# Second half of the gated state by way of DRAM, and a shorter lead of the attention

## The chip, the cores and the metric

The kernel runs on one core of a Trainium2 chip. A core has engines that run side by side, each with its own in-order queue of instructions: TensorE (PE, matrix products; its weight loads are shown as PEld), VectorE (DVE), ScalarE (ACT), GpSimd (POOL) and SyncE (SP, which here only issues DMAs). TensorE writes into PSUM, which has eight banks of 128 x 512 floats; everything else works in SBUF, and DMA engines move data between SBUF and DRAM. The metric is the device time of one execution in microseconds (us), lower is better. The kernel before takes 2796.8 us, the median of three runs (2795.94 to 2798.14).

## The reference

128 graphs of 128 nodes with 256 features pass through four residual layers. The first three are graph attention, the last is a gated graph network with three steps:

```
# layers 0, 1, 2, each with its own W and a
h = relu(layernorm(x))
Wh = h @ W
e = leaky_relu((Wh @ a1)[:, :, None] + (Wh @ a2)[:, None, :], 0.2)
x = x + elu(softmax(where(adj > 0, e, -9e15)) @ Wh)
# layer 3
h = relu(layernorm(x)); A = (adj != 0)
for i in range(3):
    aggr = einsum('bst,bsd->btd', A, h @ weight[i])
    gi = aggr @ w_ih.T + b_ih; gh = h @ w_hh.T + b_hh
    r = sigmoid(i_r + h_r); z = sigmoid(i_z + h_z); n = tanh(i_n + r * h_n)
    h = (1 - z) * n + z * h
x = x + h
```

All of it is in 32-bit floats.

## The kernel before, in words

**Groups.** The graphs are cut into 33 groups: two of 2 graphs at the ends and 31 of 4 graphs between. For each group `gat` (L661) records three attention layers and the norm ahead of the gated steps, and `gru` (L727) records the three gated steps and the output.

**Attention** (`attention`, L482): norm and scores on VectorE and ScalarE, softmax, then the sums of neighbours (`ahp`, L618) and the product with W (`hp`, L637) on TensorE. From group 2 on, the attention weights are transposed without TensorE: VectorE transposes blocks of 32 x 32, one DMA writes the tile to DRAM and four DMAs read the blocks back in their new places (`exchanged`, L429). A row of scores is spread over the partitions by two DMAs (`de`, `er`).

**A gated step** (`step`, L764). The state h is kept with features in the partitions ("feature-major"), in two halves of 128 features, k or c = 0 and 1. Half c of the new state needs six products with `whh` on the old state and six with `wc` on the aggregated state `ag` (`product`, L774, at L780), into the PSUM tiles nn, r, z and ni. ScalarE and VectorE then form r, n, z, the differences d and the new half `h` (L835 to L872). The aggregation (`agp`, L805) needs the old state the other way round, with nodes in the partitions, called `hn`; `ag` is its copy (L813). All this runs over the four graphs of the group at once, 512 columns.

**Two ways to `hn`.** For the second half (k = 1), and for both halves in groups 0, 1, 31 and 32, `node_major` (L749) lets TensorE transpose each graph's 128 x 128 piece into the PSUM tile hnp (L753), and ScalarE copies it out (L794). For the first half of groups 2 to 30 `turned_state` (L460) is used as soon as that half of h exists (L875 to L877): a block transpose on VectorE (L467), a write to DRAM (L470), four reads back (L474). The tile `hn0` of the next step is kept in the list `ahead` until that step takes it.

**PSUM.** `BANKS` (L232) gives two banks to the attention, five to the gated products and one, "tr", to `hnp` and `agp` together.

**What sets the order.** No order is written out by hand. `Plan` (L40) collects every operation with an engine, an estimated cost, a rank and its dependencies, and then plays the program through with those estimates (`issue`, L108): at each turn an engine takes, among the operations that can start within 0.1 us of the earliest (WINDOW), the one of lowest rank. An operation can't be taken while its rank is more than 6 (AHEAD) above the lowest unfinished one. The resulting order is what the engines get; on the chip each engine follows it and waits where the data isn't there yet. A DMA is an operation of SP with a cost of 0.45 us, after which its data are taken to land `lands` us later (L56); `LANDS` = 6.0 (L212) is that time for the reads of `turned_state`. Rank counts gated steps: step i of group g has rank 3g + i, its vector and scalar work a rank lower by 2 (URGENT), and layer l of the attention has 3g - lead + 2l (L485). `lead` (L916) is how many gated steps ahead of its own gated steps a group's attention begins: 8.5 for groups 0 and 1, 8.0 for the others.

Of the kernel before, what the change touches and what calls it, by code (L numbers as in the profile page):

```python
# [181 lines left out]
def kernel(  # L182
# [26 lines left out]
    B, N, D = x.shape  # L209
    KD = D // P  # L210
    G = 4
    LANDS = 6.0  # L212
    FAR = 2
    SIZES = [2] + [G] * ((B - 4) // G) + [2]
    NG = len(SIZES)
# [244 lines left out]
    def turned_state(src, dst, name, n, rank):  # L460


        tr = val(gw, "trs", [G, P], f"tr_{name}", cut=n)
        d = plan.val(
            dram, f"ds_{n}", 2, lambda: dram.tile([n, P, P], FT, tag=f"ds_{n}", name=f"d_{name}")
        )
        add("DVE", dve(n * P), rank, lambda: nc.vector.transpose(  # L467
            tr.t.rearrange("p b j -> p (b j)"), src.t[:, : n * P]
        ), reads=[src], writes=[tr], takes=[d, dst])
        load(3.0, rank, lambda: nc.sync.dma_start(d.t.rearrange("b p f -> p b f"), tr.t),  # L470
            reads=[tr], writes=[d])

        def back(j):
            load(LANDS, rank, lambda: nc.sync.dma_start(  # L474
                dst.t[j * 32 : (j + 1) * 32, : n * P].rearrange("c (m r) -> c m r", r=32),
                d.t[:, :, j * 32 : (j + 1) * 32].rearrange("b (q c) r -> c (b q) r", q=Q),
            ), reads=[d], writes=[(dst, j)])

        for j in range(Q):
            back(j)  # L480
# [246 lines left out]
    def gru(g, xt, am, hn0, h0):  # L727
# [35 lines left out]

        def step(i):  # L764
            name = f"{g}_{i}"
            rank = 3.0 * g + i
            quick = rank - URGENT
            ag = [state(f"ag{k}", f"ag_{name}_{k}") for k in range(KD)]
            hn = [
                ahead[0] if k == 0 and ahead else state(f"hn{k}", f"hn_{name}_{k}")  # L770
                for k in range(KD if i > 0 else 0)
            ]

            def product(ps, c, w, v, k, start, stop, at, takes=(), after=after):  # L774
                def fn():
                    if v is None:
                        o, m = cut(ps.t[:, :TG]), first(k)
                    else:
                        o, m = ps.t[:, :TG], v.t[:, :TG]
                    nc.tensor.matmul(  # L780
                        o, w.t[:, k, c * P : (c + 1) * P], m, start=start, stop=stop
                    )
                return add("PE", 2 * (0.005 + TG / 1200), at, fn,
                    reads=[w, h0 if v is None else v], writes=[ps], after=after, takes=takes)

            def aggregate(k):

                if i > 0:
                    hv = hn[k]
                    if k == 0 and ahead:  # L790
                        ahead.clear()
                    else:
                        hp = node_major(name, h[k], k, rank + 0.1 * k, hv)
                        add("ACT", act(TG), quick, lambda: nc.scalar.copy(  # L794
                            hv.t[:, :TG], hp.t[:, :TG]), reads=[hp], writes=[hv])
                ps = bank("tr", f"agp_{name}_{k}")
                t = ag[k]

                def part(b):
                    def fn():  # L800
                        if i > 0:
                            s = hv.t[:, b * P : (b + 1) * P]
                        else:
                            s = hn0.t[:, b, k * P : (k + 1) * P]
                        nc.tensor.matmul(  # L805
                            ps.t[:, b * P : (b + 1) * P], s, am.t[:, b, :], start=True, stop=True
                        )
                    add("PE", pe(P), rank + 0.1 * k, fn,
                        reads=[hv if i > 0 else hn0, am], writes=[(ps, b)], after=after, takes=[t])

                for b in range(n_g):
                    part(b)
                add("DVE", dve(TG), quick, lambda: nc.vector.tensor_copy(t.t[:, :TG], ps.t[:, :TG]),  # L813
                    reads=[ps], writes=[t])

            def half(c):
                at = rank + 0.2 + 0.3 * c
                cr, cz, cn = c, KD + c, 2 * KD + c
                nn, pr, pz, ni = (bank("gru", f"{v}_{name}_{c}") for v in ("nn", "r", "z", "ni"))
                wn, r, n, z, d = (state(v, f"{v}_{name}_{c}") for v in ("wn", "r", "n", "z", "d"))  # L820
                hc = state(f"h{c}", f"h_{name}_{c}")
                takes = [wn, r, n, z, d, hc, *(ag + hn if c == 0 else ())]
                begun = list(after)
                for k in range(KD):
                    early = rank + 0.1 * k if c == 0 else at
                    ops = [
                        product(nn, cn, whh, h[k], k, k == 0, k == KD - 1, early, takes),
                        product(pr, cr, whh, h[k], k, k == 0, False, early, takes),
                        product(pz, cz, whh, h[k], k, k == 0, False, early, takes),
                    ]  # L830
                    if k == 0:
                        begun += ops
                    if c == 0:
                        aggregate(k)
                add("ACT", act(TG) + 0.1, quick, lambda: nc.scalar.activation(  # L835
                    wn.t[:, :TG], nn.t[:, :TG], AF.Identity, bias=bh.t[:, cn : cn + 1]
                ), reads=[nn, bh], writes=[wn])
                for k in range(KD):
                    product(pr, cr, wc[i], ag[k], k, False, k == KD - 1, at)
                add("ACT", act(TG) + 0.1, quick, lambda: nc.scalar.activation(  # L840
                    r.t[:, :TG], pr.t[:, :TG], AF.Tanh, bias=brz.t[:, cr : cr + 1], scale=0.5
                ), reads=[pr, brz], writes=[r])
                add("DVE", dve(TG), quick, lambda: nc.vector.scalar_tensor_tensor(  # L843
                    n.t[:, :TG], r.t[:, :TG], 1.0, wn.t[:, :TG], op0=OP.add, op1=OP.mult
                ), reads=[r, wn], writes=[n])
                for k in range(KD):
                    product(ni, cn, wc[i], ag[k], k, k == 0, k == KD - 1, at, after=begun)
                add("DVE", dve(TG), quick, lambda: nc.vector.tensor_add(  # L848
                    n.t[:, :TG], ni.t[:, :TG], n.t[:, :TG]), reads=[ni, n], writes=[n])
                add("ACT", act(TG) + 0.1, quick, lambda: nc.scalar.activation(  # L850
                    n.t[:, :TG], n.t[:, :TG], AF.Tanh, bias=bi.t[:, cn : cn + 1]
                ), reads=[n, bi], writes=[n])
                for k in range(KD):
                    product(pz, cz, wc[i], ag[k], k, False, k == KD - 1, at)
                add("ACT", act(TG) + 0.1, quick, lambda: nc.scalar.activation(
                    z.t[:, :TG], pz.t[:, :TG], AF.Tanh, bias=brz.t[:, cz : cz + 1], scale=0.5
                ), reads=[pz, brz], writes=[z])

                hv = h[c]

                def difference():
                    if hv is None:
                        nc.vector.tensor_sub(cut(d.t[:, :TG]), first(c), cut(n.t[:, :TG]))
                    else:
                        nc.vector.tensor_sub(d.t[:, :TG], hv.t[:, :TG], n.t[:, :TG])

                add("DVE", dve(TG), quick, difference,
                    reads=[h0 if hv is None else hv, n], writes=[d])
                add("DVE", dve(TG), quick, lambda: nc.vector.scalar_tensor_tensor(  # L869
                    d.t[:, :TG], z.t[:, :TG], 1.0, d.t[:, :TG], op0=OP.add, op1=OP.mult  # L870
                ), reads=[z, d], writes=[d])
                add("DVE", dve(TG), quick, lambda: nc.vector.scalar_tensor_tensor(  # L872
                    hc.t[:, :TG], d.t[:, :TG], 0.5, n.t[:, :TG], op0=OP.mult, op1=OP.add
                ), reads=[d, n], writes=[hc])
                if c == 0 and i < STEPS - 1 and FAR <= g < NG - FAR:  # L875
                    ahead.append(state("hn0", f"hn_{g}_{i + 1}_0"))
                    turned_state(hc, ahead[0], f"hn_{g}_{i + 1}", n_g, quick)  # L877
                return hc

            return [half(c) for c in range(KD)]  # L880

        for i in range(STEPS):
# [32 lines left out]

    def lead(g):  # L916

        return 8.5 if g < FAR else 8.0

    for g in range(NG):  # L920
        gru(g, *gat(g))
# [37 lines left out]
```

## Time and profile before

| what | value |
|---|---|
| time, median of 3 | 2796.8 us |
| span of the profiled run | 2799.5 us |
| TensorE busy | 2744.8 us, 9789 matmul instructions |
| VectorE busy | 2188.9 us, 5680 instructions |
| ScalarE busy | 1207.8 us, 2569 instructions |
| GpSimd busy | 293.9 us, 369 instructions |
| DMA | 215.67 MB in 350398 packets, 157200 of them under 512 bytes |
| mean granted TensorE clock | 0.995 |

A busy time is the time in which at least one instruction of the engine is shown at work. A matmul's end is modelled, and consecutive matmuls overlap in the picture, so the mean duration of one is longer than what it costs in a full queue. A row "A <- B" among the waits says that A's engine stood idle until B ended; the same sign in an instruction's name stands between what it writes and what it reads. A 32-bit product counts as two matmul instructions in the profile, a transpose as one.

### The profile page before, as it was taken

The numbers are of one execution on the slowest core, as the hardware profiler recorded it, in microseconds if no ns is written. First come the engines' busy times: TensorE is split into PE (matmuls) and PEld (weight loads), VectorE is DVE, ScalarE is ACT, GpSimd is POOL, SyncE is SP. The second block draws the span as 40 slices with busy tenths as digits, with TensorE's granted clock in tenths as the row PEclk, the third lists the DMA queues.
The fourth block names the chain that finished last, engine by engine and source line by source line (L and its number), as shares of the span: only waits on it lengthen the run. The fifth ranks groups of instructions, "written<-read, shape, count | busy, mean of one in ns | idle before, by whom it ended". The sixth has DMA issues, their size and how long they took to land.

```text
span 2799.5 us, 32211 instructions
## 1 busy us (share of the span) xinstructions
PE 2744.8 (98%) x9789; PEld 1592.6 (57%) x9789; DVE 2188.9 (78%) x5680; ACT 1207.8 (43%) x2569; POOL 293.9 (10%) x369
## 2 busy tenths in 40 slices
PE   6899999999999999999999999999999999999998
PEld 4755555555555555555555555555555555555546
DVE  7879878778787878887878888788887888877544
ACT  4444444444443444444444444444444444444323
POOL 1111010010110101110100111010110110100000
PEclk9999999999999999999999999999999999999999
DMA  3113323333223333223233223232223233222210
GB/s 101 53 53 99 84 74 84 92 86 91 75 68 83 86 92 86 71 66 91 85 92 85 66 78 87 79 95 84 65 74 93 81 95 83 59 61 79 60 33 12
DMA packets 350398, 215.67 MB, mean 77 GB/s; under 512 B 157200, under 2 KB 318992, under 8 KB 350224
## 3 DMA queue, kind: packets, MB, share of 16 engines
q1 hardware_dynamic: 350224, 213.60, 28.1%
q8 instruction: 78, 1.28, 0.2%
q14 instruction: 96, 0.79, 0.1%
HBM read 124.85 MB, written 88.66 MB: 76 GB/s over the span
## 4 chain that ended last, share of the span: by engine, by line
PE 84%; DVE 9%; DMA 3%; ACT 2%; SPq 1%; issue 1%; POOL 0%; DVEq 0%; ACTq 0%
PE r L780 20%; PE z L780 20%; PE hp L637 11%; PE ni L780 10%; PE nn L780 10%; PE agp L805 5%; PE ahp L618 5%; DVE scr L506 1%; DMA d_o<-tr_o 1%; PE hnp L753 1%; DVE d L869 1%; DVE n L848 1%; DVE h L872 1%; DVE n L843 1%; DMA d_h<-tr_h 1%
## 5 line engine op out<-in xcount | busy, mean ns | idle before, releaser
L780 PE MATMUL nn<-h,whh 128*128 128x512 f32 (+1 forms) x792 | 397.8, 584 | 6.4 <-DVE h L872 6.4
L780 PE MATMUL r<-ag,wc 128*128 128x512 f32 (+1 forms) x792 | 396.6, 582 | 0.9 <-DVE ag L813 0.9
L780 PE MATMUL z<-h,whh 128*128 128x512 f32 (+1 forms) x792 | 395.9, 581 | 0.4 <-ACT r L840 0.4
L780 PE MATMUL r<-h,whh 128*128 128x512 f32 (+1 forms) x792 | 395.9, 581 | 0.0
L780 PE MATMUL z<-ag,wc 128*128 128x512 f32 (+1 forms) x792 | 394.3, 579 | 0.0
L780 PE MATMUL ni<-ag,wc 128*128 128x512 f32 (+1 forms) x792 | 393.8, 579 | 0.0
L637 PE MATMUL hp<-w,ah 128*128 128x256 f32 x1536 | 374.1, 383 | 0.7 <-ACT ah L625 0.5
L637 PEld LDWEIGHTS hp<-w,ah 128*128 128x128 f32 x1536 | 279.5, 190 | 61.9 <-issue 18.4
L506 DVE SCALAR_TENSOR_TENSOR scr<-xn,va 128x256 f32<-128x256 f32 x732 | 270.7, 424 | 29.7 <-ACT xn L498 29.4
L840 ACT ACTIVATE r<-r,brz 128x512 f32<-128x512 f32 (+1 forms) x198 | 132.9, 671 | 350.6 <-PE r L780 350.0
L780 PEld LDWEIGHTS r<-ag,wc 128*128 128x128 f32 x792 | 147.6, 190 | 181.3 <-issue 154.7
L780 PEld LDWEIGHTS z<-h,whh 128*128 128x128 f32 x792 | 150.1, 191 | 176.9 <-issue 165.4
L805 PEld LDWEIGHTS agp<-am,hn 128*128 128x128 f32 x1536 | 206.6, 192 | 73.4 <-issue 41.6
L780 PEld LDWEIGHTS r<-h,whh 128*128 128x128 f32 x792 | 151.5, 191 | 167.2 <-issue 158.7
L780 PEld LDWEIGHTS ni<-ag,wc 128*128 128x128 f32 x792 | 145.7, 190 | 149.5 <-issue 137.5
L566 ACT ACTIVATE em<-em,nmx 128x128 f32<-128x128 f32 x384 | 149.5, 391 | 187.8 <-DVE nmx L562 187.7
L780 PEld LDWEIGHTS z<-ag,wc 128*128 128x128 f32 x792 | 145.8, 190 | 148.7 <-issue 147.3
L843 DVE SCALAR_TENSOR_TENSOR n<-r,wn 128x512 f32<-128x512 f32 (+1 forms) x198 | 132.0, 667 | 119.9 <-ACT r L840 119.3
L805 PE MATMUL agp<-am,hn 128*128 128x128 f32 x1536 | 210.2, 276 | 12.7 <-DVE ag L813 8.3
L651 ACT ACTIVATE t<-hp 128x512 f32<-128x512 f32 x192 | 104.6, 594 | 267.0 <-PE hp L637 266.8
L618 PEld LDWEIGHTS ahp<-at,xn 128*128 128x128 f32 x1536 | 188.8, 194 | 47.7 <-issue 40.4
L780 PEld LDWEIGHTS nn<-h,whh 128*128 128x128 f32 x792 | 142.9, 191 | 121.3 <-issue 101.9
(91 smaller groups left out, 3508.6 us busy)
## 6 DMA issues: line engine op xcount, KB each, us to landing
er<-de SPq DMA_DIRECT2D x90, 256.0 KB, 4.1
d_at<-tr_at SPq DMA_DIRECT2D x90, 256.0 KB, 2.0
at<-d_at SPq DMA_DIRECT2D x360, 64.0 KB, 2.0
x<-in_x_dram SPq DMA_DIRECT2D x31, 512.0 KB, 3.9
d_h<-tr_h SPq DMA_DIRECT2D x31, 512.0 KB, 3.0
h<-d_h SPq DMA_DIRECT2D x124, 128.0 KB, 3.5
out_dram<-xo SPq DMA_DIRECT2D x31, 512.0 KB, 2.8
d_o<-tr_o SPq DMA_DIRECT2D x30, 512.0 KB, 5.3
```

The costliest lines, as they stand in the source:

```text
L506: add("DVE", dve(D), rank, lambda: nc.vector.scalar_tensor_tensor(scr.t, xn.t[:, b, :], 1.0 if far else rs.t[:, b : b + 1], VA[l].t[:, s, ...
L566: add("ACT", 0.42, rank, lambda: nc.scalar.activation(em.t[:, b, :], em.t[:, b, :], AF.Exp, bias=nmx.t[:, b : b + 1], accum_out=sm.t[:, b ...
L618: add("PE", pe(P), rank, lambda: nc.tensor.matmul(summed(ps, b), xn.t[:, b, k * P : (k + 1) * P], turned_weights(b), start=True, stop=True ...
L637: add("PE", pe(D), rank, lambda: nc.tensor.matmul(hp.t[:, b * D : (b + 1) * D], ah.t[:, k, c * P : (c + 1) * P], W[l].t[:, k, :], start=(k ...
L651: power = add("ACT", act(T), rank, lambda: nc.scalar.activation(t.t, hp.t, AF.Exp), reads=[hp], writes=[t])
L753: add("PE", 0.11, rank, lambda: nc.tensor.transpose(ps.t[:, b * P : (b + 1) * P], hv.t[:, b * P : (b + 1) * P], ident), reads=[hv], writes ...
L780: nc.tensor.matmul(o, w.t[:, k, c * P : (c + 1) * P], m, start=start, stop=stop)
L805: nc.tensor.matmul(ps.t[:, b * P : (b + 1) * P], s, am.t[:, b, :], start=True, stop=True)
L840: add("ACT", act(TG) + 0.1, quick, lambda: nc.scalar.activation(r.t[:, :TG], pr.t[:, :TG], AF.Tanh, bias=brz.t[:, cr : cr + 1], scale=0.5) ...
L843: add("DVE", dve(TG), quick, lambda: nc.vector.scalar_tensor_tensor(n.t[:, :TG], r.t[:, :TG], 1.0, wn.t[:, :TG], op0=OP.add, op1=OP.mult), ...
L848: add("DVE", dve(TG), quick, lambda: nc.vector.tensor_add(n.t[:, :TG], ni.t[:, :TG], n.t[:, :TG]), reads=[ni, n], writes=[n])
L869: add("DVE", dve(TG), quick, lambda: nc.vector.scalar_tensor_tensor(d.t[:, :TG], z.t[:, :TG], 1.0, d.t[:, :TG], op0=OP.add, op1=OP.mult), ...
```

## The change

The second half of the state takes the way through DRAM as well, in the same groups 2 to 30. `half(c)` calls `turned_state` for both c, and `ahead` now holds both tiles. So the 58 steps concerned have no transposes on TensorE, no copies on ScalarE, and twice the block transposes and DMAs. `ahead` is emptied before the halves are recorded, and the flag `through` says whether a step has both tiles.

The planner's numbers change with it: the write of `turned_state` is taken to land after 2.6 us (3.0 before), its reads after 2.8 (6.0 before), and a product of 512 columns to cost 0.006 us less. The attention of groups from 2 on begins 6.5 gated steps ahead in place of 8.0. The purpose is to take the remaining transposes off TensorE, with the attention's products placed where the gated steps wait for the state.

```diff
-    LANDS = 6.0
@@ turned_state
-        load(3.0, rank, lambda: nc.sync.dma_start(d.t.rearrange("b p f -> p b f"), tr.t),
+        load(2.6, rank, lambda: nc.sync.dma_start(d.t.rearrange("b p f -> p b f"), tr.t),
             reads=[tr], writes=[d])
         def back(j):
-            load(LANDS, rank, lambda: nc.sync.dma_start(
+            load(2.8, rank, lambda: nc.sync.dma_start(
@@ step
+            through = bool(ahead)
             hn = [
-                ahead[0] if k == 0 and ahead else state(f"hn{k}", f"hn_{name}_{k}")
+                ahead[k] if ahead else state(f"hn{k}", f"hn_{name}_{k}")
                 for k in range(KD if i > 0 else 0)
             ]
@@ product
-                return add("PE", 2 * (0.005 + TG / 1200), at, fn,
+                return add("PE", 2 * (0.002 + TG / 1200), at, fn,
@@ aggregate
-                    if k == 0 and ahead:
-                        ahead.clear()
-                    else:
+                    if not through:
                         hp = node_major(name, h[k], k, rank + 0.1 * k, hv)
@@ half
-                if c == 0 and i < STEPS - 1 and FAR <= g < NG - FAR:
-                    ahead.append(state("hn0", f"hn_{g}_{i + 1}_0"))
-                    turned_state(hc, ahead[0], f"hn_{g}_{i + 1}", n_g, quick)
+                if i < STEPS - 1 and FAR <= g < NG - FAR:
+                    ahead.append(state(f"hn{c}", f"hn_{g}_{i + 1}_{c}"))
+                    turned_state(hc, ahead[c], f"hn_{g}_{i + 1}_{c}", n_g, quick)
                 return hc
+            ahead.clear()
             return [half(c) for c in range(KD)]
@@ lead
-        return 8.5 if g < FAR else 8.0
+        return 8.5 if g < FAR else 6.5
```

## The prediction

> **What bounds the kernel now.** I read the page's busy times first, then the table by stretches of 100 us, then what TensorE waited for, and last the chain of waits in the middle of the run.
>
> ```profile
> PE 2744.8 (98%) x9789; PEld 1592.6 (57%) x9789; DVE 2188.9 (78%) x5680; ACT 1207.8 (43%) x2569; POOL 293.9 (10%) x369
> ```
>
> TensorE is busy in 2744.8 of 2799.5 us and VectorE in 78%. A mean doesn't say where the 54.7 us are lost; the table by stretches does (columns: stretch, length, busy time of PE, PEld, DVE, ACT and POOL with instruction counts, granted clock, DMA share, GB/s):
>
> ```profile
> 0.00:100.00 100.00, 73.96 (x337) 56.75 (x338) 76.13 (x269) 46.03 (x127) 17.67 (x30) 0.93 0.29 84
> 100.00:200.00 100.00, 91.24 (x383) 62.43 (x382) 78.22 (x233) 44.84 (x108) 13.50 (x17) 0.97 0.22 59
> 1000.00:1100.00 100.00, 100.00 (x339) 55.29 (x339) 83.05 (x216) 44.06 (x91) 11.90 (x14) 1.00 0.31 80
> 2700.00:2800.00 100.00, 90.53 (x347) 57.59 (x345) 38.72 (x72) 27.83 (x52) 0.00 (x0) 0.98 0.04 14
> ```
>
> The first 200 us lose 34.8 us and the last 100 lose 9.5. All of 200 to 2700 loses about 10 us. So from 200 us on the end is set by the amount of TensorE work, and a TensorE instruction taken away there is worth its slot. The waits of TensorE agree: the first two of these touch the state between steps, the third the attention's way through DRAM, and all are small (columns: total us, times, longest).
>
> ```profile
> PE nn L780 <- DVE h L872: 6.4, 7, 2.8
> PE agp L805 <- ACT hn L794: 4.5, 7, 0.7
> ...
> PE ahp L618 <- DMA at<-d_at: 1.2, 1, 1.2
> ```
>
> The removed work in the groups of instructions (busy us, mean ns):
>
> ```profile
> L753 PE MATMUL hnp<-ident,h 128*128 128x128 f32 x292 | 45.2, 275 | 3.4 <-DVE h L872 3.0 <-DVE ag L813 0.3
> L794 ACT COPY hn<-hnp 128x512 f32<-128x512 f32 (+1 forms) x74 | 41.5, 561 | 83.9 <-PE hnp L753 83.8
> L467 DVE STREAM_TRANSPOSE tr_hn<-h 128x512 f32<-128x512 f32 x58 | 41.3, 711 | 2.0
> ```
>
> The 275 ns are not the price of a transpose, since its modelled end overlaps the next. The chain of waits shows the slot of four (start, us):
>
> ```profile
> 1219.87 0.44 PE hnp L753 x4
> 1220.30 0.86 PE ni L780 x2
> ```
>
> 0.44 us for four, 0.11 each, with TensorE work on both sides.
>
> **What the Trainium skill says.** "Perfetto Trace Analysis", Identifying the Most-Contended Engine: matmul busy share is no measure of the distance to the limit, because the instructions are pipelined. The trace agrees: 275 ns shown, 110 ns of slot. I therefore count slots. "VectorE: DVE Perf Modes", The three transpose paths: VectorE transposes only within 32x32 blocks. That is why the new route needs the passage through DRAM to move the blocks; the trace has one such pass at 711 ns. "DMA: Bandwidth & Descriptors", Rules for kernel authors: a DMA that reads what another wrote must wait for its completion before it is issued. In the trace the four reads indeed start only 2.3 us after the write. The same page, Latency and other measured facts, gives HBM latency as 0.2 us on average and 2 us at high load, which I use only as an upper bound.
>
> **The change, part by part.**
>
> Removed from TensorE. Groups 2 to 30 (29 of them) have two steps that read a state of the step before: 58 times four transposes of the second half, 232 instructions. In the order of the built programs the transposes fall from 292 to 60 and nothing else on TensorE changes in number. 58 x 0.44 = 25.5 us, all in the stretch where TensorE is full. Removed from ScalarE: 58 copies of about 0.58 us, 34 us of an engine at 43%: nothing.
>
> Added to VectorE: 58 block transposes of 0.71 us, 41 us. It goes from 78% to (2189 + 41) / 2774 = 80%. This engine was behind none of the long TensorE waits in mid run, so I price it only through the route below.
>
> Added to the SyncE queue and DMA: 58 writes and 232 reads. The trace shows 0.38 us for a write's issue, 1.90 for four reads and 2.3 between: 4.6 us of the queue each time, 267 us in all. What is queued behind a read that waits for its write is the next write, the attention weights' round trip, loads and output; TensorE would meet them at the sums (L618). Data: runs of 32 floats, so 128-byte packets, 512 per read, 118784 in all, with 29696 in the writes. The page's 350224 packets at 28.1% of 16 engines take 36 ns each; 148480 more would be 5.3 ms of 16 engines, or 12% (estimate). The share would go to about 40%, still far from full.
>
> The new wait. The aggregation of the second half (agp, k = 1) no longer waits for a copy but for four landings. How long is the way? For the first half the trace of before shows it step by step:
>
> ```profile
> 1227.51 0.69 ACT L855 ACTIVATE z<-z,brz 128x512 f32<-128x512 f32 x1 [1.03 <-PE z L780]
> 1230.91 0.69 DVE L872 SCALAR_TENSOR_TENSOR h<-d,n 128x512 f32<-128x512 f32 x1
> 1231.64 0.71 DVE L467 STREAM_TRANSPOSE tr_hn<-h 128x512 f32<-128x512 f32 x1
> 1232.38 0.38 SPq L470 DMA_DIRECT2D d_hn<-tr_hn  x1
> 1234.70 1.90 SPq L474 DMA_DIRECT2D hn<-d_hn  x4
> ```
>
> The last z matmul's slot ends at 1227.24; z to h takes 3.43 in the median of 58 (3.74 for the second half, 4.19 in the slow tenth), h 0.72, the block transpose 0.74, write to first read 2.32 (slow tenth 3.0, longest 6.6), and the last landing comes 1.43 + 2.2 us after the first read is issued. With 0.27 ahead of z: 0.27 + 3.74 + 0.72 + 0.74 + 2.32 + 3.63 = 11.4 us. The landings themselves (least, median, most) are:
>
> ```profile
> DMA to landing us min/median/max: 1.9/2.2/4.2
> ```
>
> And how much work has TensorE in the meantime? In the changed program's order I summed the slots (0.859 for a 512-wide product, 0.431 for 256, 0.222 for 128) between the last z product of half 1 and the next step's agp of k = 1: least 11.2 us, tenth part 12.1, median 12.9, most 13.8 over 58. Half 0 has 13.8 to 18.1. So the typical margin is 1.5 us. A slow tenth of VectorE (+0.5) or of the write (+0.7) fits; both together, or a landing like 6.6, don't. My estimate: some 8 of 58 short by 0.3 us and 3 by about 1.2 us: +6 us. From below it is 0, from above 58 x 0.35 = 20 us if the heavier DMA traffic takes half of the margin away and the spread eats the rest.
>
> The planner's changed times (writes 3.0 to 2.6, reads 6.0 to 2.8) cost nothing by themselves. They state 3.05 us from write issue to read (measured 2.3) and 2.8 from last issue to landing (measured 2.2), so the plan is still on the safe side by about 1.3 us, and this is where the margin above comes from. The attention exchange is planned with 2.8 and 2.8 already, and TensorE waited for it 1.2 us in all.
>
> The lead of 6.5 in place of 8.0 adds no work. It puts the sums and products of a layer, 16 and 16 matmuls of 1.8 + 3.4 us, half a step later against the gates; without them there is only about 10 us of work to fill the 11.4. The last layer of attention ends 55 us of TensorE work ahead of its gated steps instead of 102, against some 20 us that its normalisation and exchange take: hidden. In the start-up, group 1 gets 19.9 us of work ahead of its first aggregation where it had 10.4 and TensorE stood still for 6.5; group 2 has 7.8 where it had 31, and may stand a few us. Net -3 us, between -7 and +5. The tail runs in the same form in both orders: nothing.
>
> Sum: 2796.8 - 25.5 - 3 + 6 = 2774 us.
>
> **The rivals.**
>
> - **The wait takes the transposes' place.** For it: only 1.5 us of margin, and one instruction on an in-order engine. Against: the attention exchange is planned as tightly and shows 1.2 us of waiting. 0.35 us x 58 = 20 in place of 6: 2788.
> - **DMA becomes the limit, slower than before.** With a third more busy time every landing may come later. At +1.1 us per leg (within the page's 2 us at high load) a trip is 2.2 late, 0.7 beyond the margin: 58 x 0.7 = 41, 2768 + 41 = 2809. Against: 40% busy, and landings of 2.2 us beside loads of 512 KB already.
> - **More is won.** No new wait, the 6.5 us of the start gone, and half of the 10 us of small waits in mid run too, since the single bank of aggregation and transposes no longer alternates between two uses: 2797 - 25.5 - 6.5 - 5 = 2760.
>
> **How the numbers follow.** Forecast (2766 to 2782) 0.66; wait in its place 0.15; slower 0.08; more won 0.11. The likeliest gives 2774. From 2762 to 2791 leaves out the slower case, and the edges of two others, about 2 in 10. Faster by over 0.2% (below 2791.2): 0.66 + 0.11 + three fifths of 0.15 = 0.86; within 0.2%: 0.06; slower: 0.08.
>
> **What would show it.** Right: 60 hnp matmuls, PE busy near 2719 us, DVE near 2230 us; mid-run stretches still at 99 to 100; waits of agp for hn<-d_hn under 10 us; DMA share near 40%. Wrong: stretches in mid run at 97 or less with agp waiting for DMA (the first rival); landings of hn at 3 us or more in the median (the second); more than 40 us lost in the first 200 us (the lead).

## The result

The changed kernel takes 2775.0 us, the median of four runs (2774.29 to 2775.59), against 2797.12 us before in the same comparison (four runs, 2795.94 to 2798.14). The ratio is 0.9921 with a 95% interval of 0.9904 to 0.9938. The forecast was 2774. The time is nearly exactly the forecast one, but the sum that gave it is not the sum that the chip made: of its three terms only the first was right, and the errors of the others cancelled. Most of this section and the next are about that.

**The profile after.** The page's busy times:

```profile
PE 2710.1 (98%) x9557; PEld 1565.2 (56%) x9557; DVE 2199.0 (79%) x5738; ACT 1171.7 (42%) x2511; POOL 288.2 (10%) x369
```

9789 - 9557 = 232 matmul instructions fewer on TensorE, 58 more on VectorE, 58 fewer on ScalarE, as the diff says. VectorE's busy time rose by only 10 us: its 58 transposes did add 41 us, but others took less time or overlapped more in this order. The table by stretches, same columns as before:

```profile
0.00:100.00 100.00, 75.72 (x363) 58.40 (x364) 78.12 (x275) 48.24 (x133) 17.57 (x30) 0.93 0.27 79
100.00:200.00 100.00, 96.35 (x379) 62.05 (x379) 75.54 (x217) 44.10 (x97) 11.94 (x15) 1.00 0.19 57
200.00:300.00 100.00, 84.85 (x305) 49.72 (x304) 84.59 (x231) 42.74 (x95) 11.36 (x15) 0.95 0.37 102
1000.00:1100.00 100.00, 99.50 (x331) 54.63 (x331) 85.56 (x226) 42.16 (x93) 11.12 (x14) 1.00 0.37 100
```

and the stretch from 200 to 300 of the kernel before, for the third row:

```profile
200.00:300.00 100.00, 98.49 (x371) 58.61 (x370) 87.89 (x235) 48.76 (x105) 12.53 (x16) 1.00 0.34 95
```

The first 200 us lose 27.9 us in place of 34.8, but the third hundred now loses 15.2 where it lost 1.5. In mid run TensorE is at 99 to 100% as before. What TensorE waited for (total us, times, longest):

```profile
PE nn L780 <- DMA h<-d_h: 9.0, 2, 8.4
PE r L780 <- DVE ag L811: 8.4, 14, 0.8
...
PE agp L803 <- DMA hn<-d_hn: 0.3, 1, 0.3
```

The last row is the wait that the prediction priced at 6 us: it is 0.3 in this view, and 1.5 us in three steps by the finer count below, which also sees what a matmul's modelled end hides. The first two rows weren't in the prediction as such. The landings of the way, 464 reads now (least, median, most), are a little later than before:

```profile
DMA to landing us min/median/max: 1.8/2.4/5.3
```

**A finer count than busy time.** A matmul's shown end is modelled, so a stretch with 100% busy can still have lost time. I therefore took the start times of all TensorE matmuls from the trace and subtracted from each interval between two starts the slot of the first (0.429 us for half a product of 512 columns, 0.216 for 256, 0.111 for 128, and in proportion for the 48 instructions of 384). What is left over is called a hole here. Time that a matmul loses because the clock runs at half speed is counted as a hole too. Slots, holes, the time to the first matmul and that after the last add up to the span. "Start" is the first 300 us, "tail" the last 190.

| kernel | slots | holes, start | holes, mid run | holes, tail | ends | span |
|---|---|---|---|---|---|---|
| before | 2707.4 | 44.9 | 26.7 | 7.9 | 12.5 | 2799.5 |
| changed | 2681.8 | 51.4 | 19.0 | 8.4 | 12.1 | 2772.7 |
| difference | -25.6 | +6.5 | -7.7 | +0.5 | -0.4 | -26.8 |

The profiled execution of before took 2801.3 us, 4.2 above its median, and that of the changed kernel 2774.5, 0.5 below, which is why the spans differ by 26.8 and the medians by 22.1. Some of the holes of before may belong to that one execution. The transposes are worth what was said, the start got worse where it was to get better, and the middle got better where it was to get worse.

The 26.7 us of before are not spread evenly. 14.5 of them lie between 300 and 700 us: five stops of 0.8 to 3.0 us, and 2.9 us of half speed after the longest. From 700 us on about 0.6 us is lost in each 100. Busy time shows only 9.2 of the 26.7 us.

### The profile page after: what moved, and what is told of

Same layout as the page of the kernel before. It is cut to its first block, busy times and chain, and to the rows that moved or that the text cites. A ratio compares the mean times of both kernels' runs of the same rounds, so it can differ in the third digit from the quotient of the medians.

```text
span 2772.7 us, 32377 instructions
## 1 busy us (share of the span) xinstructions
PE 2710.1 (98%) x9557; PEld 1565.2 (56%) x9557; DVE 2199.0 (79%) x5738; ACT 1171.7 (42%) x2511; POOL 288.2 (10%) x369
## 2 busy tenths in 40 slices
DMA packets 503519, 246.08 MB, mean 89 GB/s; under 512 B 280624, under 2 KB 472112, under 8 KB 503344
## 3 DMA queue, kind: packets, MB, share of 16 engines
q1 hardware_dynamic: 503344, 244.03, 33.6%
## 4 chain that ended last, share of the span: by engine, by line
PE 84%; DVE 11%; ACT 2%; DMA 1%; issue 1%; SPq 0%; POOL 0%; ACTq 0%; DVEq 0%; POOLq 0%
PE r L780 21%; PE z L780 21%; PE ni L780 11%; PE hp L636 10%; PE nn L780 9%; PE ahp L617 6%; PE agp L803 5%; DVE em L547 2%; DVE xo L652 1%; DVE xo L654 1%; ACT em L565 1%; DVE ag L811 1%; DVE d L867 1%; DVE h L870 1%; DVE d L863 1%
## 5 line engine op out<-in xcount | busy, mean ns | idle before, releaser
L636 PE MATMUL hp<-w,ah 128*128 128x256 f32 x1536 | 360.5, 380 | 2.5 <-ACT ah L624 2.4
L636 PEld LDWEIGHTS hp<-w,ah 128*128 128x128 f32 x1536 | 290.5, 191 | 100.7 <-issue 61.5
L833 ACT ACTIVATE wn<-nn,bh 128x512 f32<-128x512 f32 (+1 forms) x198 | 132.9, 671 | 359.1 <-PE nn L780 358.9
L617 PEld LDWEIGHTS ahp<-at,xn 128*128 128x128 f32 x1536 | 188.8, 194 | 47.6 <-issue 42.1
```

What stands on the lines that cost most here:

```text
L617: add("PE", pe(P), rank, lambda: nc.tensor.matmul(summed(ps, b), xn.t[:, b, k * P : (k + 1) * P], turned_weights(b), start=True, stop=True ...
L636: add("PE", pe(D), rank, lambda: nc.tensor.matmul(hp.t[:, b * D : (b + 1) * D], ah.t[:, k, c * P : (c + 1) * P], W[l].t[:, k, :], start=(k ...
```

## The experiments

Each is given with its ratio to the kernel before, timed on the same chip, since the chips of different comparisons differ by a few us. The interval of each ratio is about 0.0015 to each side. The changed kernel has 0.9921.

**Which part brings the gain: the transposes or the lead?** First the second half back on TensorE, all else as changed:

```diff
-                if i < STEPS - 1 and FAR <= g < NG - FAR:
+                if c == 0 and i < STEPS - 1 and FAR <= g < NG - FAR:
@@ step
-            through = bool(ahead)
+            through = len(ahead)
-                ahead[k] if ahead else state(f"hn{k}", f"hn_{name}_{k}")
+                ahead[k] if k < len(ahead) else state(f"hn{k}", f"hn_{name}_{k}")
-                    if not through:
+                    if k >= through:
```

> The changed kernel with the second half back on TensorE (58 x 4 transposes, 58 copies), lead 6.5 and all planner numbers kept. Theory (TensorE slots are the gain): 25.5 us above the changed kernel, 2798 to 2806, so no faster than the kernel before; the start stays as bad as in the changed kernel. Rival (the lead and the planner's numbers made the gain): 2770 to 2785, near the changed kernel. 292 hnp matmuls.

Measured: 2785.5 us, ratio 0.9957 (0.9942 to 0.9972). That is far from the theory's range and half a us above the rival's: it has every transpose and yet is 12 us faster than before, and only 10 us slower than the changed kernel. Then the kernel before with nothing but the lead changed:

```diff
-        return 8.5 if g < FAR else 8.0
+        return 8.5 if g < FAR else 6.5
```

> The kernel before with one number changed: lead 6.5 in place of 8.0 for groups from 2 on. It has all 292 transposes and the planner's old landing times. Theory (e1 owes its 12 us to the lead): 2783 to 2789, the mid-run holes of TensorE under 8 us in place of 27 and the start about 7 us longer. Rival (the new landing times did it): 2793 to 2803.

Measured: 2784.4 us, ratio 0.9943 (0.9928 to 0.9958), as the theory said. The lead alone is worth 0.57%, 16 us. Its table by stretches shows where (TensorE is the second number of a row):

```profile
0.00:100.00 100.00, 72.66 (x350) 55.41 (x351) 76.75 (x271) 46.52 (x127) 17.76 (x30) 0.95 0.27 79
100.00:200.00 100.00, 97.68 (x392) 63.68 (x392) 77.19 (x220) 45.64 (x103) 12.13 (x15) 1.00 0.19 56
200.00:300.00 100.00, 86.97 (x308) 51.61 (x307) 85.20 (x233) 44.52 (x104) 11.32 (x15) 0.93 0.35 95
1000.00:1100.00 100.00, 100.00 (x341) 55.72 (x340) 82.11 (x215) 43.63 (x95) 10.70 (x14) 1.00 0.31 85
```

The same loss between 200 and 300 is there without the second way, so it belongs to the lead. In the row of mid run the busy share says 100 for this kernel and for the one before. Over the whole of mid run it shows 0.1 us lost against 9.2, and the holes say 2.8 us against 26.7. The shorter lead removes both the stops between 300 and 700 us and the small holes after them. The order may be a part of the reason: the first use of the second half's new state comes 6.5 us of TensorE work (median of 58) after the last z product, where it came 4.8 us after it at lead 8.0, and the way from that product to the state takes 0.27 + 3.74 + 0.72 = 4.7 us. But only 7 of the 26.7 us stand ahead of products nn<-h, so this is not the whole of it.

**What does the way through DRAM still cost?** The second half with no transposition at all: the aggregation reads the feature-major half as if it were the other. The transposition of this half is left out of the computation.

```diff
-                    ahead.append(state(f"hn{c}", f"hn_{g}_{i + 1}_{c}"))
-                    turned_state(hc, ahead[c], f"hn_{g}_{i + 1}_{c}", n_g, quick)
+                    if c == 1:
+                        ahead.append(hc)
+                    else:
+                        ahead.append(state(f"hn{c}", f"hn_{g}_{i + 1}_{c}"))
+                        turned_state(hc, ahead[c], f"hn_{g}_{i + 1}_{c}", n_g, quick)
```

> The second half has neither transposes nor the way through DRAM: the aggregation of k = 1 reads the feature-major half itself, so the transposition of this half is left out of the computation. It costs what the way of the changed kernel costs beyond its hidden part. Theory (the way is hidden): 2767 to 2775, no more than 8 us below the changed kernel. Rival (a wait or the DMA traffic of the way takes part of the gain): 2745 to 2762.

Measured: 2763.7 us, ratio 0.9878 (0.9864 to 0.9893), between the two. The way costs about 11 us (12 by the ratios) beyond what is hidden; mid-run holes are 5.8 us here and 19.0 in the changed kernel. The changed kernel's own trace shows where they sit. Of its 19.0 us, 12.2 stand ahead of products r<-ag. The timeline at one of them (start, us; the bracket gives the engine's idle time and what ended it):

```profile
1393.63 1.05 PE L803 MATMUL agp<-am,hn 128*128 128x128 f32 x8
...
1394.82 0.69 DVE L576 TENSOR_TENSOR em<-em,ri 128x512 f32<-128x512 f32 x1
...
1395.38 1.02 PE L780 MATMUL nn<-h,whh 128*128 128x512 f32 x2
1395.54 0.71 DVE L441 STREAM_TRANSPOSE tr_at<-em 128x512 f32<-128x512 f32 x1
1396.18 0.65 DVE L811 COPY ag<-agp 128x512 f32<-128x512 f32 x1
...
1396.88 1.13 PE L780 MATMUL r<-ag,wc 128*128 128x512 f32 x2 [0.48 <-DVE ag L811]
```

The aggregation's slots end at 1394.5. Its copy (L811) starts at 1396.18, because VectorE works off a softmax and a block transpose of the attention first. TensorE has only two products, 1.72 us, between the aggregation and the first use of the copy; the order of the program says so for the median of 58 steps. In the kernel without the way there are 3.43 us. The independent products that could stand here are spent ahead of the aggregation, to cover the way. So this copy went to ScalarE in the steps concerned (both engines read PSUM here: ScalarE copied `hn` out of it before, VectorE `ag`):

```diff
-                add("DVE", dve(TG), quick, lambda: nc.vector.tensor_copy(t.t[:, :TG], ps.t[:, :TG]),
-                    reads=[ps], writes=[t])
+                if k == 1 and through:
+                    add("ACT", act(TG), quick, lambda: nc.scalar.copy(t.t[:, :TG], ps.t[:, :TG]),
+                        reads=[ps], writes=[t])
+                else:
+                    add("DVE", dve(TG), quick, lambda: nc.vector.tensor_copy(t.t[:, :TG], ps.t[:, :TG]),
+                        reads=[ps], writes=[t])
```

> The changed kernel, but in the steps that take both halves through DRAM the copy of the second aggregation goes to ScalarE in place of VectorE. Theory (the way's remaining cost is that this copy stands in VectorE's queue behind the softmax while only 1.7 us of TensorE work is left behind the aggregation): r<-ag waits fall from 12 us to under 4, time 2763 to 2769. Rival (the landings or the DMA traffic cost the 11 us between this kernel and the one without the way): 2772 to 2778.

Measured: 2764.5 us, ratio 0.9872 (0.9857 to 0.9887), 10 us below the changed kernel (14 by the ratios) and level with the one that has no way. The holes ahead of r<-ag fall from 12.2 us to 0.0, those of mid run from 19.0 to 8.4. Its waits for landings are still small, 3.3 us in this view and 5.1 by the holes:

```profile
PE agp L803 <- DMA hn<-d_hn: 3.3, 6, 1.3
```

In its timeline the copy follows the aggregation at once:

```profile
1391.72 0.59 ACT L812 COPY ag<-agp 128x512 f32<-128x512 f32 x1
1391.83 0.69 DVE L576 TENSOR_TENSOR em<-em,ri 128x512 f32<-128x512 f32 x1
...
1393.24 1.02 PE L780 MATMUL r<-ag,wc 128*128 128x512 f32 x2
```

The planner made another order for this kernel too (12.9 us of work for the way in nearly all steps), so the edit is not the copy alone. But the order still leaves only 1.72 us in the median between the aggregation and the first use of its copy. What is new is when the copy starts: counted from the start of the aggregation's last matmul it was 0.37 us in the median and 2.04 in the slow tenth of the changed kernel, and it is 0.31 in both here. The holes at that place are gone, and the way's cost with them.

**What is the lead for?** The changed kernel at the old lead:

```diff
-        return 8.5 if g < FAR else 6.5
+        return 8.5 if g < FAR else 8.0
```

> The changed kernel with the lead of 8.0 for groups from 2 on. Theory (attention placed half a step later fills the 11.4 us of the way): TensorE has only 11.7 us of work in the median between the last z product and the aggregation of k = 1 and the order has holes elsewhere, so waits of about 0.5 to 1.5 us in each of 58 steps: 2800 to 2850, slower than before. Rival (the lead matters only for the start): 2765 to 2780, with the start of the kernel before.

Measured: 2932.7 us, ratio 1.0485 (1.0469 to 1.0501), far beyond the range given. Direction as the theory said, size and place not:

```profile
PE nn L780 <- DVE h L870: 84.5, 50, 2.2
PE z L780 <- ACT r L838: 23.4, 20, 3.4
PE agp L803 <- DVE ag L811: 18.9, 39, 7.9
```

TensorE doesn't wait for landings. It waits for the new state itself, on VectorE. (7.9 us of the third row are one stop in the start.) In this order the first use of the second half stands 4.3 us of work after the last z product (median), where the changed kernel has 6.9, and the z activation to the block transpose takes 5.23 us on VectorE in place of 4.32. Of the attention's products none stands between the two points in most of the 58 steps, where the changed kernel has 3.5 us of them in the median. Of 177.6 us of holes in mid run 98.5 stand ahead of nn<-h.

Does a half step of phase matter, or the shorter lead? The kernel before once more:

```diff
-        return 8.5 if g < FAR else 8.0
+        return 8.5 if g < FAR else 7.5
```

> The kernel before with lead 7.5 for groups from 2 on: half a step off as 6.5 is, but a whole step longer. If what closes TensorE's holes is where in a step the attention falls (its order leaves 6.0 us of work in the median between the last z product and the first use of the second half, 6.9 at lead 6.5 and 4.8 at 8.0, against 4.7 us that this half takes): mid-run holes of 5 to 15 us, 2785 to 2792. If a shorter lead does it: holes as before, 2795 to 2800.

Measured: 2820.9 us, ratio 1.0077 (1.006 to 1.0093). Both expectations missed: it is slower than lead 8.0. (Of the figures in the expectation, 6.9 us is that of the changed kernel; the kernel before at lead 6.5 has 6.5.) The holes of mid run are 42.1 us, with 17.7 ahead of the transposes:

```profile
PE hnp L753 <- DVE ag L813: 15.0, 8, 2.9
```

Here the transposes wait until the copy has emptied the one PSUM bank that they share with the aggregation. So neither phase nor length is the rule. The leads 6.5, 7.5 and 8.0 leave 2.8, 42.1 and 26.7 us of holes, each by the order that the planner settles into.

**What are the planner's landing times for?** The old ones in the changed kernel:

```diff
-        load(2.6, rank, lambda: nc.sync.dma_start(d.t.rearrange("b p f -> p b f"), tr.t),
+        load(3.0, rank, lambda: nc.sync.dma_start(d.t.rearrange("b p f -> p b f"), tr.t),
-            load(2.8, rank, lambda: nc.sync.dma_start(
+            load(6.0, rank, lambda: nc.sync.dma_start(
```

> The changed kernel in which the planner takes the write to land after 3.0 us and the reads after 6.0, as before; same operations and same DMAs, another order. Theory (the honest landing times are what lets the aggregation follow the way closely): the plan wants 3.6 us more between half 1 and its aggregation, for which there is no work; the ready gated products stand behind other instructions and TensorE idles: 2790 to 2860. Rival (the planner's number is harmless because the chip goes by semaphores): 2770 to 2785.

Measured: 2867.1 us, ratio 1.0253 (1.0236 to 1.027), a little beyond the range. The waits:

```profile
PE agp L803 <- DVE ag L811: 57.6, 54, 2.0
```

The data lie there; the second aggregation waits for the copy of the first to empty the bank "tr". In a quarter of the 58 steps the two aggregations stand within 1.7 us of TensorE work of each other in this order, down to none, where the changed kernel has at least 2.6, and more than 5 in three quarters. The Trainium skill says in "Perfetto Trace Analysis", Matmuls, that independent groups should rotate through different PSUM banks so that the copy of one overlaps the next. The trace agrees: these 54 waits of 57.6 us are what the one shared bank costs in this order. No run here gives the aggregations a second bank.

**Is the DMA system near a limit?** Each way reads its blocks a second time, into a tile nobody uses (`extra`, two buffers):

```diff
+        def again(j):
+            load(2.8, rank, lambda: nc.sync.dma_start(
+                extra.t[j * 32 : (j + 1) * 32, : n * P].rearrange("c (m r) -> c m r", r=32),
+                d.t[:, :, j * 32 : (j + 1) * 32].rearrange("b (q c) r -> c (b q) r", q=Q),
+            ), reads=[d], writes=[(extra, j)])
+        for j in range(Q):
+            again(j)
```

> The changed kernel in which each of the 116 ways reads its four blocks a second time, into a tile that nobody uses: 464 more reads of 64 KB with 128-byte packets, right behind the real ones. Theory (DMA isn't the limit): 2774 to 2782, landings of hn at 2.2 to 2.8 us in the median. Rival (DMA traffic makes the landings late and they are what TensorE pays for): 2790 to 2830.

Measured: 2806.4 us (20 executions, 2797.3 to 2812.6), ratio 1.0022 (1.0015 to 1.0029). The theory falls, and the time is the rival's: 31 us (28 by the ratios) more than the changed kernel. Here TensorE does wait for landings:

```profile
PE agp L813 <- DMA hn<-d_hn: 32.7, 28, 2.5
```

The extra reads put both traffic and issues on the way. To part them, the same order with extra reads of 4 KB:

```diff
-                extra.t[j * 32 : (j + 1) * 32, : n * P].rearrange("c (m r) -> c m r", r=32),
-                d.t[:, :, j * 32 : (j + 1) * 32].rearrange("b (q c) r -> c (b q) r", q=Q),
+                extra.t[j * 32 : (j + 1) * 32, :32], d.t[0, :32, j * 32 : (j + 1) * 32],
```

> The kernel that reads every way twice, in the same order of instructions, but each extra read moves 4 KB in 32 packets in place of 64 KB in 512. As many DMAs in SyncE's queue, hardly any traffic. If the 31 us of the doubled reads are traffic: back to 2774 to 2780. If they are the queue (extra issues ahead of the next write): 2795 to 2808. Both: in between.

Measured: 2782.4 us, ratio 0.9947 (0.9932 to 0.9962), in between.

```profile
PE agp L812 <- DMA hn<-d_hn: 13.1, 13, 1.6
```

The two kernels have the same order, so 24 us (21 by the ratios) are traffic, and about 7 are the queue with the planner's new order. Late landings are only a small part of it: counted from their issue, the reads land in 2.5 us in the median with the double traffic and in 2.4 without. The way of the second half is longer as a whole. From the z activation to the last landing it takes 11.3 us in the changed kernel (mean of 58), 12.2 with the small extra reads and 12.8 with the full ones.

The small reads add 0.9 us: the write is issued 0.3 later after the start of its block transpose, and the first read 0.6 later after the write. Full reads add another 0.6 us, half of it again ahead of the write's issue. With the 0.27 us ahead of z, the way stands against 12.9 us of work in the median of all three orders. So the first addition mostly uses up the margin of 1.4 us, and the second, though smaller, is paid almost in full. Why traffic holds up the issue of a write is not shown.

**Can the start be had back?** Group 2 alone at the old lead:

```diff
-        return 8.5 if g < FAR else 6.5
+        return 8.5 if g < FAR else 8.0 if g == 2 else 6.5
```

> The changed kernel with the lead of group 2 alone at 8.0, the others from 3 on at 6.5. Theory (the start's loss of 6.5 us is the state of group 2 arriving late after only 7.8 us of work): 31.9 us of work stand there now, the 8.6 us wait for h goes, 2765 to 2770. Rival (the start is bound by group 0 and 1, the wait moves on): 2773 to 2777.

Measured: 2774.9 us, ratio 0.9909 (0.9894 to 0.9924): no clear gain. The wait moved, as the rival said; the 8.4 us for the state of group 2 are gone, and in their place stands the wait for the one bank, which the kernel before had in its start too:

```profile
PE agp L803 <- DVE ag L811: 6.5, 1, 6.5
```

Holes in the start: 51.3 us against 51.4. With groups 2 and 3 at 7.0 and the copy on ScalarE, the same:

```diff
-        return 8.5 if g < FAR else 6.5
+        return 8.5 if g < FAR else 7.0 if g < 4 else 6.5
```

> The kernel with the second aggregation's copy on ScalarE, and lead 7.0 for groups 2 and 3. The steady part stays as it is (TensorE has 12.9 us of work for the way in the median); if the start's loss falls by the 6 us that TensorE waits for the state of group 2: 2758 to 2762; if it moves to another wait, as with group 2 alone at 8.0: 2763 to 2767.

Measured: 2763.6 us, ratio 0.9879 (0.9865 to 0.9894), level with the kernel without this edit; 54.0 us of holes in the start.

**A version that beats both.** The copies of both aggregations on ScalarE in all groups, with group 2 at lead 8.0:

```diff
-                add("DVE", dve(TG), quick, lambda: nc.vector.tensor_copy(t.t[:, :TG], ps.t[:, :TG]),
+                add("ACT", act(TG), quick, lambda: nc.scalar.copy(t.t[:, :TG], ps.t[:, :TG]),
@@ lead
-        return 8.5 if g < FAR else 6.5
+        return 8.5 if g < FAR else 8.0 if g == 2 else 6.5
```

> The changed kernel with the copies of both aggregations on ScalarE in all groups, and lead 8.0 for group 2. Frees 131 us of VectorE and adds 113 us to ScalarE. If VectorE's queue is what costs the rest: 2757 to 2763. Against it: a tenth of the steps have only 11.2 us of work for the way of 11.5, so landings may be waited for: 2764 to 2772.

Measured: 2757.8 us (2757.0 to 2758.9), ratio 0.9857 (0.9842 to 0.9872), the fastest of all. Busy times:

```profile
PE 2709.0 (98%) x9557; PEld 1568.9 (57%) x9557; DVE 2088.1 (76%) x5540; ACT 1279.4 (46%) x2709; POOL 293.3 (11%) x369
```

VectorE gave 111 us to ScalarE, which had room. Of the holes, mid run has 8.3 us and the start 46.1. The feared waits for landings did not come: all holes ahead of agp in mid run are 1.1 us. Against the kernel with one copy moved the gain is 4 us by the ratios, and the start has 4.7 us of holes less; no run separates the second copy from the lead of group 2.

The holes of all kernels but the two above. Half speed makes 7.9 us of those in mid run at lead 7.5, 16.9 at lead 8.0, 16.2 with the old landing times and 6.4 with the reads twice; in the other kernels of the table it makes none there.

| kernel | slots | start | mid run | tail | span |
|---|---|---|---|---|---|
| second half on TensorE | 2707.4 | 52.0 | 3.4 | 8.1 | 2783.3 |
| before, lead 6.5 | 2707.4 | 51.3 | 2.8 | 8.4 | 2782.1 |
| before, lead 7.5 | 2707.4 | 50.6 | 42.1 | 9.1 | 2822.3 |
| no way | 2681.8 | 52.3 | 5.8 | 7.9 | 2760.8 |
| lead 8.0 | 2681.8 | 47.7 | 177.6 | 8.5 | 2928.0 |
| old landing times | 2681.8 | 52.6 | 107.5 | 10.0 | 2864.8 |
| copy on ScalarE | 2681.8 | 50.8 | 8.4 | 8.4 | 2762.5 |
| reads twice | 2681.8 | 50.8 | 53.4 | 8.9 | 2807.2 |
| small extra reads | 2681.8 | 52.5 | 25.5 | 8.1 | 2780.3 |
| group 2 at 8.0 | 2681.8 | 51.3 | 18.0 | 9.7 | 2773.8 |
| copy on ScalarE, groups 2, 3 at 7.0 | 2681.8 | 54.0 | 8.7 | 8.4 | 2764.6 |
| both copies on ScalarE | 2681.8 | 46.1 | 8.3 | 8.0 | 2755.7 |

## Why the prediction was right, and where its steps failed

- **Transposes, -25.5 us: right.** The slots of TensorE fell by 25.6. Taken alone, with the lead at 6.5 on both sides and no way in their place, they are worth 21.9 us of time (2785.5 to 2763.7).
- **The lead, "adds no work", net -3 us: failed, in two places.** In the start the sign was wrong: +6.5 us. The 6.5 us stop ahead of group 1 did go, but "may stand a few us" for group 2 was 8.4, with shorter stops ahead of it. (Half speed followed both stops and makes little difference between the kernels: 20.5 us of it in the first 300 before, 23.9 after.) And the sum had no term for mid run at all, where the lead removes 24 us of holes (26.7 to 2.8). The step behind this was the reading "All of 200 to 2700 loses about 10 us", which took busy time for work and those 10 us for fixed. Busy time shows 9 of the 24 us, and the lead removes them. The other 15 were hidden below the modelled ends of matmuls, although the prediction had said itself that such an end overlaps the next instruction. (Its first citation says that the trace agrees with the page. It does in that busy share misleads; but the page has pipelined instructions look smaller in the trace, and here they look longer, 275 ns for 110 of slot.)
- **The new wait, +6 us: a wait did come, but in another place, and larger.** The way was put at 11.4 us and the work beside it at 12.9. For the second half the changed kernel's trace gives 0.27 + 8.87 (z activation to the fourth read's issue) + 2.4 (landing) = 11.5 us, and TensorE lost 1.5 us to landings. But the step looked at the aggregation only. Work that is used up ahead of it is missing behind it, where the copy has to pass VectorE's queue: 12.2 us, and 16.2 in mid run in all against the lead alone (2.8 to 19.0). "This engine was behind none of the long TensorE waits in mid run, so I price it only through the route below" is the sentence that failed: the route doesn't end at the landing. The prediction's own line had VectorE's h behind a wait of 2.8 us, and that one stands in mid run, at 532 us.
- **The planner's numbers "cost nothing by themselves": right in the direction taken, blind in the other.** With the old ones the change would have been 2.5% slower than before.
- **DMA: the share was put too high, the danger too low.** About 40% was forecast, the page says 33.6%: 503519 packets, 153121 more, took (0.336 x 2772.7 - 0.281 x 2799.5) x 16 = 2320 us of engine time, 15 ns each in place of 36. The 36 ns was the mean of packets of all sizes; in the trace's records one of 128 bytes takes 12.9 ns and one of 512 bytes 28.7. But the rival that makes DMA the limit was nearer than its 0.08: doubling the reads makes the kernel slower than before.
- **The total: right by cancelling.** The three terms gave -22.5 and the medians -22.1. In the spans it is -25.6 (slots) + 6.5 (start) - 24 (lead, mid run) + 16 (way) = -27, measured -26.8. The misses in mid run, -24 forecast as 0 and +16 as +6, come to -14 together, that in the start to +9.5. That leaves 4.5 us, and the spans are that much further apart than the medians because of the slow profiled execution of before. That 2774 was met to 1 us is luck.

Of its signs, TensorE's busy time fell to 2710.1 us (2719 was said), VectorE's is 2199.0 (2230), and the others on its list for "right" came true except the DMA share.

What stays open is why the planner's order closes the holes at lead 6.5 and not at 7.5 or 8.0. The traces show which wait each order leaves, not a rule that would tell it ahead.

## What to carry to other kernels

Count a full engine's loss by the intervals between its starts and not by its busy share: here busy time showed 9 us of loss in a mid run that had 27, and closing those holes paid about as much as the transposes. Look also at when they occur: half of them came early, before 700 us. When a longer wait is covered by pulling independent work ahead of it, look at the next hand-over behind it, since that work is no longer there; moving the copy that stood in a busy engine's queue to a less busy one was worth 10 us. Where a planner orders the work, its assumed durations and leads are part of the change: one of them put back turned -0.8% into +4.8%.

## What was not expected of the hardware

- **128-byte packets are cheap on the DMA engines, and still not free.** One takes 12.9 ns in the changed kernel and 12.7 with the reads doubled. Yet the doubled traffic made each way of the second half 0.6 us longer than the same number of small reads did, and cost TensorE 21 to 24 us.
- **A TensorE stop of 8 us is followed by half speed, and so were much shorter ones.** The chain of waits of the changed kernel after the stop ahead of group 2 (start, us; two instructions are one product):

```profile
236.10 2.04 PE nn L780 x2
238.14 1.71 PE r L780 x2
239.85 0.89 PE z L780 x2
240.74 0.86 PE nn L780 x2
```

A product takes 0.86 to 0.89 us from the third on; the first two cost 2.0 us more than that together. The Trainium skill describes it in "TensorE: Matmul & The Clock Gate", What's actually happening: an idle window of about 3.4 us puts the array at half its clock. Here the stop was 8.4 us, and the granted clock of the stretch from 200 to 300 us reads 0.95. But the clock's records have half speed from 229.5 to 239.8 us, so it began 2.0 us into the stop. The stop at 532 us in the kernel before shows the same with less:

```profile
534.72 2.08 PE L780 MATMUL nn<-h,whh 128*128 128x512 f32 x2 [2.83 <-DVE h L872]
536.59 1.91 PE L780 MATMUL r<-h,whh 128*128 128x512 f32 x2
```

Half speed runs from 533.9 to 540.7 us there and cost 2.9 us beyond the stop. In the kernel with the old landing times even stops of 1.6 us were followed by it, while in the one with lead 8.0 several of 2.4 us were not. So stops shorter than the page's 3.4 us did it in these traces, and they give no threshold of their own.
